# Inner rows of the gate and up products moved into the output stage of a transformer block: pieces between attention's products, Silu built from Exp, operands in two steps, layernorm in place

## The chip, the core and the metric

The kernel runs on one core of a Trainium2 chip. Its engines each work through their own instructions in order: TensorE (PE) for matmuls, VectorE (DVE) and ScalarE (ACT) for elementwise work and for reading the matmul banks (PSUM), GpSimd (POOL) for elementwise work, SyncE (SP) mainly for issuing transfers. The metric is the device time of one launch in microseconds (us); all data is float32.

## What is computed

Two sequences of 1024 tokens with 1024 features go through attention and a gated feed-forward block. Both are modulated by vectors that come from a small conditioning input. Cut to what matters here:

```python
h = layernorm(x) * (1 + ca) + sa
qkv = clip(h @ Wqkv.T, -8, 8)            # q and k are normalised, then 32 heads of 32
probs = softmax(q @ k.T * scale + alibi, causal)
x = x + ga * ((probs @ v) @ Wout.T)      # the output stage
h = layernorm(x) * (1 + cb) + sb         # called h2 in the kernel
gate = (h @ Wg.T) * ag                   # 2752 inner rows
up = (h @ Wu.T) * au
out = x + gb * (((silu(gate) * up) @ Wd.T) * ad)
```

## The kernel before

The inner dimension of 2752 is split. Five blocks of 512 (2560) run in the gate-and-up stage through two nested levels of a seven-product scheme (Strassen-Winograd). What is left, 192 inner rows, one full slice of 128 and one of 64, is called the rest. It is done with plain products, stored in `rest_dram`, and added in the down stage.

Tokens go in pairs of 128-row tiles: batch b, pair j from 0 to 3, eight pairs (b, j) in all.

**Order of the stages.** PE's instructions stand in program order (`matmul`, L763, while `pinned` is set). The other engines' instructions are placed by the framework's scheduler, so a DMA or a vector operation may stand ahead of where it is written.

1. Projections of batch 0 (`projections`, L943).
2. Attention of both batches (`attention`, L1029), interleaved with dense work (`dense_work`, L1500) by `together` (L1164). `together` walks through attention's units (96 of them for each batch) and runs dense work as long as its estimated time is below `share` (L1535). While batch 0's attention runs, the dense work is the projections of batch 1 with `side` (L1505), which takes one step of `down_weights` (L1204: load, four sums on POOL, store) at each of the products from the 24th on. While batch 1's attention runs, the dense work is the output stage of pairs (0,0) to (0,3), (1,0) and (1,1). `DENSE1` (L1356) is the estimated dense time spread over batch 1's attention.
3. After attention: the output stage of (1,2) and (1,3), together with all rest rows (`rest_rows`, L1377), and `second_batch` (L1335), which forms for each j the sums and differences of both batches' h2 that the gate-and-up stage needs, and sends them to `bop_dram` through `inner_b` (L1188).
4. Gate and up (L1824), then down (L1949).

**A unit of attention.** `scores` (L1052) issues four score matmuls (tile sc), then exponentials on ACT (L1085) that write p, and masks on POOL (L1089). `weigh` (L1095) issues the products with v (tile av) two units later, and adds p into the running sum on DVE or POOL (L1117). `settle` (L1119) multiplies the sum with ones. Scores have one buffer for each half, so the next unit's scores wait for the exponentials of this one.

**The output stage.** `operand` (L1244) loads the reciprocal softmax sums (rb) and four blocks of the attention output (aoA), multiplies them on DVE and POOL (L1264) and forms S1 to S4 (L1265 to L1269). `output` (L1274) calls it for a pair when the pair begins, unless it was made before. Then `seven` (L841) issues seven products of four matmuls, in chunks of two. `read` (L1296) takes each bank: copies on ACT (L1299), adds on DVE (L1305, L1307), products and adds into xr on POOL (L1308, L1309). The rows x1 are stored (L1314), normalised into a second tile xn (`normalize`, L719; the write is L747), transposed through a bank in four groups (`turned`, L861) and written, scaled, to h2 by DVE (L869).

**Pieces.** Transposes are put into a list (`Todo`, L876) and taken from it one at a time between chunks of the next pair. A piece takes a bank from `Banks.turn` (L784). During attention there is one such bank, shared with `settle`; `fresh` (L781) says whether it may be taken again. Each piece counts as 0.6 us for `together`.

**Rest rows.** For each pair three products of eight matmuls (tile rest, weights restw): gate of the slice of 128, up of the slice of 128, and both of the slice of 64 side by side. ACT applies Silu with the scale (L1392, L1393), DVE multiplies (L1396, L1399), SP stores (L1403, L1404). The h2 of six of the pairs is loaded back from memory for it (tile hl, `fetch`, L1550), and for `second_batch` too. Their weights are written after `output(0, ...)` in the program; the scheduler placed their loads ahead of the output weights (wB_o, wT_o).

Of the kernel before, what the change touches and what calls it, by code (L numbers as in the profile page):

```python
# [480 lines left out]
def kernel(  # L481
# [394 lines left out]
    class Todo:  # L876
# [18 lines left out]
        def add(self, go):  # L895
            self.list.append(go)

        def run(self, n, all_=False):
            self.place()
            for _ in range(min(n, len(self.list))):  # L900
                if not all_ and not self.banks.fresh():
                    return
                self.list.pop(0)(self.banks.turn())
                yield TURN
# [339 lines left out]
    def operand(b, j, ap_, own=None):  # L1244

        qb, y0 = 2 * j * P // QB, 2 * j * P % QB
        rb = ap_.tile([P, KC, 2 * P], FP, tag="rb", name=f"rb_{b}_{j}")
        for g in range(4):
# [7 lines left out]
                bufs=2 if q == "A21" and own is None else None,  # L1256
# [3 lines left out]
        for m, kh, q, eng in (  # L1260
            (0, 0, "A11", nc.vector), (0, 1, "A12", nc.gpsimd), (1, 1, "A22", nc.vector), (1, 0, "A21", nc.gpsimd),
        ):
            nc.sync.dma_start(a[q], ao_dram[b][qb][:, ds(kh * 4, 4), ds(y0 + m * P, P)])
            eng.tensor_mul(a[q], a[q], rb[:, ds(kh * 4, 4), ts(m, P)])  # L1264
# [5 lines left out]
        return a  # L1270
# [3 lines left out]
    def output(b, js, pools, banks, bt, todo, keep, made={}, q0=1):  # L1274
# [9 lines left out]
        for j in js:  # L1284
# [3 lines left out]
            a = made.get((b, j)) or operand(b, j, ap_)  # L1288
# [5 lines left out]
            part_t = {}  # L1294

# [15 lines left out]
            yield from seven(lambda q, i: a[q][:, i, :], bt, banks, read, todo.places(q0, 1), 2)  # L1311
# [3 lines left out]
            xn = []  # L1315
            for m in range(2):
                t_ = tkp.tile([P, D], FP, tag="xn", name=f"xn_{b}_{qts[m]}", bufs=2)
                xn.append(t_)
            todo.first(normalize(xs, xn, sm, f"f{b}_{j}"), b == 1 and j >= NJ // 2 - 1)
            h2 = keep(b, j)  # L1320
            for m in range(2):
                for g in range(2):
# [10 lines left out]
                    todo.add(go)  # L1333

# [21 lines left out]
    LEAD, DENSE0, DENSE1 = 16.0, 370.0, 136.0  # L1356
# [20 lines left out]
    def rest_rows(pairs, rest_w, pool, psp, tiles):  # L1377

        n1 = REST[1][1]
        ib = 4 * NSB  # L1380
        for b, j in pairs:
            hl = tiles[b, j].rearrange("p k h t -> p k (h t)")
            ps = []
            for r in range(3):
                bank = psp.tile([P, 512], FP, tag="rp", name=f"rest_{b}_{j}_{r}")[:, 0:256]
                for k in range(KC):
                    matmul(bank, rest_w[r][:, k, :], hl[:, k, :], start=(k == 0), stop=(k == KC - 1))
                ps.append(bank)
                yield 3.4
            sg = pool.tile([P, 2, 256], FP, tag="rsg", name=f"rsg_{b}_{j}")  # L1390
            ac = pool.tile([P, 2, 256], FP, tag="rac", name=f"rac_{b}_{j}")
            nc.scalar.activation(sg[:, 0], ps[0], AF.Silu, scale=vt[:, R_AG + ib : R_AG + ib + 1])  # L1392
            nc.scalar.activation(  # L1393
                sg[64 : 64 + n1, 1], ps[2][0:n1], AF.Silu, scale=vt[0:n1, R_AG + ib + 1 : R_AG + ib + 2]
            )
            nc.vector.scalar_tensor_tensor(  # L1396
                ac[:, 0], ps[1], vt[:, R_AU + ib : R_AU + ib + 1], sg[:, 0], ALU.mult, ALU.mult
            )
            nc.vector.scalar_tensor_tensor(  # L1399
                ac[64 : 64 + n1, 1], ps[2][64 : 64 + n1],  # L1400
                vt[64 : 64 + n1, R_AU + ib + 1 : R_AU + ib + 2], sg[64 : 64 + n1, 1], ALU.mult, ALU.mult,
            )
            nc.sync.dma_start(rest_dram[0][:, b, j], ac[:, 0].rearrange("p (h t) -> p h t", h=2))  # L1403
            nc.sync.dma_start(  # L1404
                rest_dram[1][0:n1, b, j], ac[64 : 64 + n1, 1].rearrange("p (h t) -> p h t", h=2)
            )
# [645 lines left out]
```

## Time and profile before

| what | us |
|---|---|
| median of 3 runs | 2902.21 (2901.19 to 2909.03) |
| the profiled execution, by the same clock as the runs | 2896.01 |
| its span, first to last instruction | 2894.3 |
| PE busy, share of the span | 2702.2, 93% |
| DVE, POOL, ACT busy | 1453.0, 1296.8, 685.2 |

The page shows the span in 40 equal slices of 72.4 us; each digit is a busy share in tenths, and PEclk the granted PE clock.

```profile
## 2 busy tenths in 40 slices
PE   6999999999997787878989999999999998999998
DVE  5766535665543356665554453454535346444442
ACT  1322244444443555545110011010101100000000
POOL 3312033345655565556457364464735541222342
PEclk9999999999998899999999999999999999999999
DMA  9878763756557444342687667585766659555542
```

Slices 13 to 19 are attention of batch 1 with the output stage between its products (about 907 to 1380 us); slices 20 to 22 hold the work behind it and the start of gate and up. The groups of instructions give the durations of the operations concerned: line, engine, operation, tiles, shape, count, then busy time and mean ns of one, then the idle time of the engine ahead of them.

```profile
L763 PE MATMUL rest<-hl,restw 128*128 128x256 f32 x288 | 65.3, 384 | 0.0
L763 PE MATMUL rest<-h2t,restw 128*128 128x256 f32 x96 | 21.6, 380 | 0.5 <-DVE rac L1396 0.5
L1392 ACT ACTIVATE rsg<-rest,vt x8: 473/473/474, 1400.7 to 1546.3; 128x256 f32<-128x256 f32 x8
L1396 DVE SCALAR_TENSOR_TENSOR rac<-rest,vt,rsg x8: 471/481/484, 1403.7 to 1556.5; 128x256 f32<-128x256 f32 x8
L1138 DVE RECIPROCAL rc<-rc x4: 935/947/953, 572.4 to 1389.2; 128x128 f32<-128x128 f32 x4
L869 DVE TENSOR_SCALAR h2t<-bank,modt 128x128 f32<-128x128 f32 x128 | 43.7, 402 | 25.0 <-PE bank L766 24.8
```

Each float32 matmul leaves two records, so 384 records of rest are 192 matmuls, 24 products. (In the three lines with "x8:" and "x4:" the numbers are the least, median and greatest ns, then the first and last start in us.)

### The profile page before, as it was taken

How to read it: one execution, taken by the hardware profiler on the slowest of the kernel's cores; microseconds unless marked ns; L12 is line 12 of the kernel's file. 1: busy time of each engine (PE TensorE's matmuls, PEld its weight loads, DVE VectorE, ACT ScalarE, POOL GpSimd, SP SyncE). 2: the span in 40 equal slices, each digit the busy share in tenths (PEclk: the TensorE clock that was granted, in tenths of full speed). 3: DMA queues.
4: the chain of work that ended last, by engine and by line, in shares of the span. 5: the costliest groups of instructions: out<-in, count | busy, mean ns of one | idle time of the engine just before them, and what ended most of it. 6: DMA issues, size and time to landing. Idle time of an engine off the chain costs nothing.

```text
span 2894.3 us, 29930 instructions
## 1 busy us (share of the span) xinstructions
PE 2702.2 (93%) x10271; PEld 1330.2 (46%) x10271; DVE 1453.0 (50%) x2285; ACT 685.2 (24%) x1523; POOL 1296.8 (45%) x1270
## 2 busy tenths in 40 slices
PE   6999999999997787878989999999999998999998
PEld 2444433333332222222655444444444446888776
DVE  5766535665543356665554453454535346444442
ACT  1322244444443555545110011010101100000000
POOL 3312033345655565556457364464735541222342
PEclk9999999999998899999999999999999999999999
DMA  9878763756557444342687667585766659555542
GB/s 342 311 270 311 284 219 117 236 181 220 191 164 236 130 153 134 124 124 77 208 262 241 211 225 235 169 285 160 268 190 206 229 169 286 158 146 146 158 144 81
DMA packets 377573, 579.14 MB, mean 200 GB/s; under 512 B 21590, under 2 KB 278712, under 8 KB 366276
## 3 DMA queue, kind: packets, MB, share of 16 engines
q1 hardware_dynamic: 363928, 556.12, 59.2%
q10 hardware_dynamic: 13484, 21.02, 2.2%
q8 instruction: 84, 1.38, 0.2%
q14 instruction: 77, 0.63, 0.1%
HBM read 411.89 MB, written 165.17 MB: 199 GB/s over the span
## 4 chain that ended last, share of the span: by engine, by line
PE 43%; DMA 4%; DVE 3%; issue 3%; POOL 3%; ACT 1%; SPq 0%; POOLq 0%; DVEq 0%; ACTq 0%
PE gx L1824 7%; PE ux L1824 7%; PE dx L1949 7%; PE gy L1824 6%; PE uy L1824 6%; PE dy L1949 5%; PE bank L763 1%; DMA bt<-bop_B 1%; DMA bop_T<-inner_T 1%; PE sc L763 1%; ACT p L1085 1%; DMA wuA<-in_L_ffn_Wu_dram 1%; PE rest L763 0%; PE av L763 0%; DVE asS L1778 0%
## 5 line engine op out<-in xcount | busy, mean ns | idle before, releaser
L1085 ACT ACTIVATE p<-sc,kw 128x128 f32<-128x128 f32 (+3 forms) x1024 | 421.6, 513 | 394.9 <-PE sc L763 376.7
L763 PE MATMUL bank<-wT,a 128*128 128x512 f32 x768 | 353.6, 603 | 12.0 <-DVE wT L832 6.8
L1117 POOL TENSOR_TENSOR p<-p,p 128x1024 f32<-128x1024 f32 (+3 forms) x128 | 262.1, 2048 | 183.4 <-PE av L763 157.5
L1117 DVE TENSOR_TENSOR p<-p,p 128x1024 f32<-128x1024 f32 (+3 forms) x192 | 246.2, 1291 | 153.4 <-POOL p L1089 97.3
L763 PE MATMUL bank<-wB,a 128*128 128x512 f32 x576 | 262.5, 601 | 1.2 <-DVE raw L982 0.6
L763 PE MATMUL sc<-cq,ck 32*128 32x512 f32 (+3 forms) x1536 | 194.5, 548 | 56.4 <-ACT p L1085 56.1
L1089 POOL TENSOR_SCALAR_AFFINE_SELECT p<-p 128x256 f32<-128x256 f32 x256 | 139.3, 556 | 200.8 <-ACT p L1085 194.7
L763 PEld LDWEIGHTS bank<-wT,a 128*128 128x128 f32 x768 | 140.0, 192 | 186.2 <-issue 168.9
L763 PE MATMUL av<-p,cv 128*32 128x512 f32 (+3 forms) x1536 | 173.2, 514 | 17.2 <-POOL p L1089 17.2
L763 PEld LDWEIGHTS bank<-wB,a 128*128 128x128 f32 x576 | 104.5, 190 | 145.0 <-issue 123.6
L763 PEld LDWEIGHTS sc<-cq,ck 32*128 32x128 f32 x1536 | 64.5, 186 | 193.6 <-ACT p L1085 103.0
L1824 PE MATMUL gy<-bt,sig 128*128 128x512 f32 x280 | 132.4, 595 | 10.7 <-DMA bt<-bop_B 5.7
L1824 PE MATMUL uy<-bt,siu 128*128 128x512 f32 x280 | 131.6, 592 | 0.0
L1824 PE MATMUL gx<-bt,sig 128*128 128x512 f32 x280 | 131.6, 592 | 0.0
L1824 PE MATMUL ux<-bt,siu 128*128 128x512 f32 x280 | 131.6, 592 | 0.0
L763 PEld LDWEIGHTS av<-p,cv 128*32 128x32 f32 x1536 | 34.0, 110 | 138.7 <-issue 80.7
L1824 PEld LDWEIGHTS gy<-bt,sig 128*128 128x128 f32 x280 | 52.4, 190 | 80.8 <-issue 71.1
L763 PE MATMUL bank<-wB_o,aoA 128*128 128x512 f32 x128 | 68.3, 667 | 18.7 <-DVE aoS L1266 17.7
L1824 PEld LDWEIGHTS uy<-bt,siu 128*128 128x128 f32 x280 | 53.2, 190 | 67.0 <-issue 65.8
L1824 PEld LDWEIGHTS ux<-bt,siu 128*128 128x128 f32 x280 | 53.2, 190 | 67.0 <-issue 65.5
L1824 PEld LDWEIGHTS gx<-bt,sig 128*128 128x128 f32 x280 | 53.2, 190 | 67.0 <-issue 65.7
L1824 PE MATMUL ux<-bt,wuS 128*128 128x512 f32 x160 | 75.2, 592 | 0.0
(415 smaller groups left out, 4467.9 us busy)
## 6 DMA issues: line engine op xcount, KB each, us to landing
bt<-bop_T SPq DMA_DIRECT2D x140, 512.0 KB
bt<-bop_B SPq DMA_DIRECT2D x99, 512.0 KB
a<-hop SPq DMA_DIRECT2D x20, 1792.0 KB
wm<-in_L_wmod_dram SPq DMA_DIRECT2D x48, 512.0 KB
wB<-in_L_attn_Wqkv_dram SPq DMA_DIRECT2D x21, 1024.0 KB
aq_S<-act_S SPq DMA_DIRECT2D x16, 1280.0 KB
qk<-qs SPq DMA_DIRECT2D x16, 1024.0 KB
act_S<-asS SPq DMA_DIRECT2D x30, 512.0 KB
```

What stands on the lines that cost most here:

```text
L763: return in_order(nc.tensor.matmul(*args, **kw_))
L1085: last_exp[0] = nc.scalar.activation(p[:, g, lo:hi], sp[:, g, lo:hi], AF.Exp, bias=kw[:, d, h_ : h_ + 1])
L1089: last_mask[0] = nc.gpsimd.affine_select(out=p[:, :, 0:P], in_=p[:, :, 0:P], pattern=[[0, 2], [1, P]], compare_op=ALU.is_ge, fill=0.0, bas ...
L1117: adders[b](half, jb).tensor_add(dst, dst, ps[half][:, :, 0:n])
L1824: nc.tensor.matmul(ps.rearrange("p (j t) -> p j t", j=NJ), ins[mat][qa][:, c2, :], bt[:, :, c2, :], start=(q in ("P1", "P2", "P5") and c2 ...
L1949: nc.tensor.matmul(bank[c_], ins[qa][:, s, :], wt[qb_][:, s, :], start=(q in ("P1", "P2", "P5") and s == 0), stop=(s == NSB - 1), skip_gro ...
```

## The change

- `rest_rows` goes. `rest_pieces` puts the three products of a pair into the list of pieces, behind the pair's transposes, with 3.5 us each in the estimate, and with two entries that take no bank and only issue the elementwise work. All eight pairs do it; six are in the part of the output stage that is dense work. The products read h2 from where it was just written.
- Silu is no longer called there. ACT takes the gate from the bank with its scale (Identity) and applies Exp to its negative; DVE limits, adds one, takes the reciprocal and multiplies twice. The scaled up rows go through a tile of the constants, `sc`, that is free by then. Exp, Ln and Identity are in the table that attention uses.
- `operand` has two steps. During a pair's third product the next pair's loads are issued, during its seventh its elementwise work. Block A22 gets a second buffer, as A21 had.
- The rows are normalised in place: xn is xr. The pool tok has four buffers of xr instead of three and two of xn.
- The rest weights are allocated ahead of the operand pool and loaded ahead of the output stage, on SP.
- `side` begins at the 12th product instead of the 24th; `DENSE1` goes from 136 to 190.
- After attention, the pieces left of (1,1) run with three more banks, then (1,2) and (1,3) are done one behind the other. The h2 of batch 0's pairs and of (1,0), (1,1) is still loaded for `second_batch`.

```diff
 class Todo:
-        def add(self, go):
-            self.list.append(go)
+        def add(self, go, us=TURN):
+            self.list.append((go, us))
         def run(self, n, all_=False):
             self.place()
-            for _ in range(min(n, len(self.list))):
+            while n and self.list:
+                go, us = self.list[0]
+                if us is None:
+                    go()
+                    self.list.pop(0)
+                    continue
                 if not all_ and not self.banks.fresh():
                     return
-                self.list.pop(0)(self.banks.turn())
-                yield TURN
+                self.list.pop(0)
+                go(self.banks.turn())
+                n -= 1
+                yield us
...
 def operand(b, j, ap_, own=None):
...
-                bufs=2 if q == "A21" and own is None else None,
+                bufs=2 if q in ("A21", "A22") and own is None else None,
...
+        for m, kh, q, eng in blocks:
             nc.sync.dma_start(a[q], ao_dram[b][qb][:, ds(kh * 4, 4), ds(y0 + m * P, P)])
+        yield
+        for m, kh, q, eng in blocks:
             eng.tensor_mul(a[q], a[q], rb[:, ds(kh * 4, 4), ts(m, P)])
...
 def output(...):
+            def ahead(e):
+                if e == 2 and nxt not in made and not step and (nxt[0], 2 * nxt[1] * P // QB) in settled:
+                    step[0] = operand(*nxt, ap_)
+                    next(step[0])
+                elif e == 6 and step and nxt not in made:
+                    next(step[0])
...
-            yield from seven(lambda q, i: a[q][:, i, :], bt, banks, read, todo.places(q0, 1), 2)
+            yield from seven(lambda q, i: a[q][:, i, :], bt, banks, read, todo.places(q0, 1, ahead), 2)
...
-            xn = []
-            for m in range(2):
-                t_ = tkp.tile([P, D], FP, tag="xn", name=f"xn_{b}_{qts[m]}", bufs=2)
-                xn.append(t_)
+            xn = xs
...
+            if rest is not None:
+                rest_pieces(b, j, todo, h2, *rest)
...
-    LEAD, DENSE0, DENSE1 = 16.0, 370.0, 136.0
+    LEAD, DENSE0, DENSE1 = 16.0, 370.0, 190.0
...
+    def rest_pieces(b, j, todo, h2, rest_w, pool):
+        n1 = REST[1][1]
+        hl = h2.rearrange("p k h t -> p k (h t)")
+        tiles = {}
+        def scaled(dst, ps, vec, r, rows_):
+            ib = vec + 4 * NSB + r
+            nc.scalar.activation(dst, ps, AF.Identity, scale=vt[rows_, ib : ib + 1])
+        def product(w, bank):
+            ps = bank[:, 0:256]
+            for k in range(KC):
+                matmul(ps, w[:, k, :], hl[:, k, :], start=(k == 0), stop=(k == KC - 1))
+            return ps
+        def gate(ps, r, lo, hi):
+            g, e = (pool.tile([P, 256], FP, tag=nm, name=f"{nm}_{b}_{j}_{r}") for nm in ("rg", "re"))
+            scaled(g[hi], ps[lo], R_AG, r, lo)
+            nc.scalar.activation(e[hi], g[hi], AF.Exp, scale=-1.0)
+            tiles[r] = g, e
+        def up(ps, r, hi):
+            scaled(urow[hi], ps[hi], R_AU, r, hi)
+        def act(r, hi, n):
+            g, e = tiles[r]
+            nc.vector.tensor_scalar(e[hi], e[hi], FAR, 1.0, ALU.min, ALU.add)
+            nc.vector.reciprocal(e[hi], e[hi])
+            nc.vector.tensor_mul(g[hi], g[hi], e[hi])
+            nc.vector.tensor_mul(g[hi], g[hi], urow[hi])
+            nc.sync.dma_start(rest_dram[r][0:n, b, j], g[hi].rearrange("p (h t) -> p h t", h=2))
+        every, lo, hi = slice(0, P), slice(0, n1), slice(64, 64 + n1)
+        urow = sc.rearrange("p k c -> p (k c)")
...
+        todo.add(lambda bank: gate(product(rest_w[0], bank), 0, every, every), 3.5)
+        todo.add(lambda bank: up(product(rest_w[1], bank), 0, every), 3.5)
+        todo.add(lambda: act(0, every, P), None)
+        todo.add(last, 3.5)
+        todo.add(lambda: act(1, hi, n1), None)
...
-                if 7 * n + e >= 24:
+                if 7 * n + e >= 12:
                     next(steps, None)
...
-            for n, k in (("oga", 1), ("tok", 3), ("opart", 1), ("osmall", 1), ("ao", 1))
+            for n, k in (("oga", 1), ("tok", 4), ("opart", 1), ("osmall", 1), ("restw", 1), ("ao", 1))
...
-        yield from output(0, range(NJ), *out_args, made)
-        right["w"] = rest_weights(rwp, nc.sync)
+        out_args.append((rest_weights(rwp, nc.sync), rwp))
+        yield from output(0, range(NJ), *out_args)
...
+    banks.others = banks.others + [rps.tile([P, 512], FP, tag=f"rq{i}", name=f"rq{i}") for i in range(3)]
...
-    with_turns(rows((0, 0), (1, 0)))
+    alone(todo.run(len(todo.list), True))
     fetch(1, 1)
-    def between():
-        yield from rows((0, 1))
-        second(0)
-        yield from rows((1, 1))
-    together(
-        between(), output(1, range(NJ // 2, NJ), *out_args, made, 3), lambda a: 0.6 * OUT_US / 2 * a / 20.6
-    )
+    second(0)
+    alone(output(1, range(NJ // 2, NJ), *out_args[:5], 5, out_args[6]))
+    second(1)
     in_range(rest_pool, rps)
     fetch(0, 2)
-    second(1)
     fetch(0, 3)
-    with_turns(rows((0, 2), (1, 2)))
     second(2)
-    alone(rows((0, 3), (1, 3)))
+    alone(todo.run(len(todo.list), True))
```

## The prediction

> **What bounds the kernel now.** I read three views: busy time by stretches, for the stages; the timeline of TensorE (PE) in two of them; the waits of PE. The cuts come from the timeline: 897 is the last matmul before the output stage, 1380 the end of attention, 1546 the first matmul of the gate-and-up stage.
>
> ```profile
> 895.00:916.00 21.00, 3.30 (x20) 0.71 (x18) 4.67 (x6) 2.62 (x5) 3.54 (x3) 0.68 0.98 268
> 916.00:1380.00 464.00, 381.51 (x2161) 123.12 (x2161) 257.79 (x356) 239.45 (x576) 278.44 (x250) 0.93 0.43 134
> 1380.00:1546.00 166.00, 153.88 (x579) 105.91 (x578) 91.77 (x178) 22.32 (x35) 76.28 (x64) 0.98 0.76 243
> ```
>
> Columns: stretch, length, busy PE, weight loads, VectorE (DVE), ScalarE (ACT), GpSimd (POOL), PE clock, DMA share, GB/s. In 464 us of attention over batch 1 no engine is full. In the 166 us behind it PE is nearly full, and DMA at 0.76.
>
> ```profile
> PE sc L763 <- ACT p L1085: 46.8, 41, 3.7
> PE bank L763 <- DVE aoS L1266: 17.7, 1, 17.7
> PE av L763 <- POOL p L1089: 17.2, 7, 5.1
> PE bank L763 <- DVE h2t L869: 15.2, 2, 8.6
> ```
>
> These are all of PE's long waits in 907 to 1379. The first is the attention loop itself: scores of a unit cannot start until ACT has read those of the unit before. The second is one stall at the stage's start.
>
> ```profile
> 1348.83 1.22 PE L763 MATMUL sc<-cq,ck 32*128 32x512 f32 x8
> 1349.98 0.43 PE L763 MATMUL av<-p,cv 128*32 128x128 f32 x8
> 1352.57 1.78 PE L763 MATMUL sc<-cq,ck 32*128 32x512 f32 x8 [2.17 <-ACT p L1085]
> ```
>
> A unit of 512 columns with no filler takes 3.7 us from scores to scores, of which PE works about 2. With one output chunk of 1.98 us (1346.91 is one) it takes about 4.0.
>
> ```profile
> 1392.50 10.52 PE L763 MATMUL rest<-hl,restw 128*128 128x256 f32 x48
> 1499.53 10.53 PE L763 MATMUL rest<-hl,restw 128*128 128x256 f32 x48
> 1546.12 1.88 PE L1824 MATMUL gx<-bt,wgA 128*128 128x512 f32 x4
> ```
>
> A pair's three inner-row products cost PE 10.5 us, 3.45 each. Twenty-four of them, 83 us, fill half of the stage behind attention.
>
> **What the Trainium skill says.** *TensorE: Matmul & The Clock Gate*, "What's actually happening": the PE clock falls to half after an idle window of about 3.4 us. The trace agrees: clock 0.68 around the stall, and the first chunk after it takes 3.67 us against 1.98. *ScalarE: Activation LUTs*, "What ACT_TABLE_LOAD costs": 1283 ns, with a drain 2.66 us; the trace shows 1.28 for the load. *VectorE: DVE Perf Modes*, "First, the fixed hardware budget": reciprocal is an iterative divide; here 128x128 takes 947 ns against about 285 for a tensor-tensor of that shape.
>
> **Part 1, the start of the output stage.** PE stands from 898.3 to 915.98. On SP's queue the last down-weight stores (888), operand loads (901 to 906.7) and wB_o (906.95) go one behind another; DVE's S2 ends at 915.9. With `side` at 12 the down-weight steps are over twelve products earlier. In the built order of the changed kernel the operand loads of (0,0) stand ahead of the last chunk loads, and wB_o follows the last stores of v, so it can issue at about 897.5, when the last projection matmul frees its space. Its load and the next are then the limit: 4 to 5 us. PE resumes at about 902.5 instead of 916: 13 us gained. Bounds: 6, if 1.5 MB more of rest weights and the 7 MB of wB_o crowd each other (DMA share is 0.98 here already), and 18, the whole stall with its slow first chunk. The earlier POOL work lies under batch 0's products, where PE is 91 to 99% busy and POOL 39 to 65% (stretches of 80 us from 440 to 840): nothing.
>
> **Part 2, pieces inside attention.** The built order gives the placement. Of 24 products 14 stand ahead of the last attention matmul: four pairs of batch 0 and two products of (1,0). Between score groups (101 of them) 28 intervals had no filler and 17 will have none; 12 of the 14 pieces have an interval to themselves, 2 share one with a chunk.
> - An interval of a piece alone: 1.07 + 1.00 + 3.45 = 5.5 us against 3.65, so 12 x 1.85 = 22 us.
> - Two on top of a chunk: 2 x 3.45 = 7 us.
> - Intervals with two chunks go from 8 to 13, with one from 61 to 53: 5 x 1.9 less 8 x 0.35 = 7 us.
> - ACT: six operations of 0.47 for each pair where two stood later; they come when the piece ends, under PE's next groups: nothing. DVE: `act` has two reciprocals of 256 columns, about 1.85 each (twice 947 less overhead, an estimate), and six small operations, about 6 us for each pair. DVE has 206 us free, but the softmax sums, the bank reads and the L869 reads that free the single shared bank queue behind: 4 us.
> - Operands in two steps: DVE waits 13.1 us at L1264 in the middle of the stage, 7.68 of it on the chain at 1247. Loaded a pair's half ahead this goes, but PE shows little of it: minus 5.
> - Layernorm in place: the write-back now waits for the x1 store, and SP, in order, puts that behind chunk loads. The normalisation is issued behind the next pair's first products: +1 to +2.
> Sum: attention gets 36 us longer, and I take off 4 for a clock above 0.93 as long gaps close: 32. Bounds: 15, if the 46.8 us of waits on ACT swallow most of the 48.3 us of pieces; 55, if nothing is swallowed and DVE adds 7.
>
> **Part 3, behind attention.** Ten products stay: 34.5 us instead of 82.8. Counted from attention's end:
> - rest of (1,1) and one piece: 15 us. Then nothing fills: last matmul to normalised rows took 7.7 us (1392.5 to 1400.2); plus 2 for the x1 store, 1.5 for the rows, 6 for four groups of reads at 1.37. Pieces of (1,1) run from 32 to 42.5. The operand of (1,2) is ready at about 34 (softmax sums at 10, rb loads at 24).
> - two pairs of products, 48.2, two groups of transposes, 2.4, waits of 3: up to 96. Before, this point was 1499.4, or 119.
> - pieces of (1,2) 10.4, beside the last normalisation. Before, that took from 1499.4 to 1510.27, with 3.84 us of table loads in it; now 7, plus 2 for the store, 1.5 and 6: 16.5. Pieces of (1,3): gate-and-up starts at 123.
> - its weights issue on ACT's queue when the last output matmul frees their space (1499.62 before), its sixth bt tile was issued by 1523.5, 24 us later: no stall of its own. SP has the stores of third and second pair, four weight tiles and bt still to issue. I expect it just late for the seventh tile: 4 us.
> So 127 against 166: 39 gained. Bounds: 20, if DMA binds (40.35 MB moved in those 166 us at 243 GB/s; in 127 us it would be 318, and the best 20 us slices show 323 to 329), and 48, the pieces alone.
>
> **Sum.** -13 + 32 - 39 = -20 us: 2876 against the profiled execution's 2896.01 (span 2894.3). The median of the runs shown is 2902.21, 6 above it; on that scale 2882. Gate-and-up and down stages keep their work.
>
> **Rivals.**
> - Everything is absorbed: attention +18, start -15, tail -48: 2857. For it, 82 us of PE waits in the loop; against it, a piece of 3.45 us does not fit a gap of 1.6.
> - DMA takes PE's place behind attention: tail -20, total -1: 2901. For it, share 0.76 and one SP queue in order with 40 MB; against it, some stores may slip under the first gate-and-up products.
> - Slower. Attention's loop stretches by the full length of the pieces: ACT reads a piece from the shared bank only in its turn behind exponentials, PE, in order, waits for that bank with transposes and sums behind it, and DVE's divides hold the reads. Attention +55, tail -30, start -10: +15, 2917. It decides from 50 us of stretching at a tail of 39. For it, PE already lost 15.2 us on that bank (L869); against it, 11 intervals that stood empty take pieces.
>
> **How the numbers follow.** A measurement tells about 0.3%, 9 us, from no change. Forecast (-20, plus or minus 12) 0.50; absorbed 0.14; DMA 0.17; slower 0.19. Faster: 0.95 of the first, all of the second, 0.4 of the third, 0.05 of the fourth: 0.69. Slower: a quarter of the third, three quarters of the fourth: 0.18; the same 0.13. The range 2854 to 2914 cuts about half of each outer case; most of the chance has one sign, so it stands alone.
>
> **What would show it.** Right: the first output matmul within 8 us of the last projection matmul; attention from there 25 to 40 us longer; attention's end to the first gate-and-up matmul near 127 us, with a PE gap of about 17 us ahead of the pieces of (1,1); no table load before gate-and-up. Wrong: PE waits on ACT or DVE for the shared bank above 30 us in attention; gate-and-up waiting for bt or weights by over 10 us; a start still held by wB_o.

## The result, and the profile after

The changed kernel takes 2884.05 us, median of 9 runs (2880.18 to 2893.61), beside 2905.58 for the kernel before, also 9 runs. The ratio is 0.9928, with a 95% interval of 0.9913 to 0.9942: about 21 us faster, 17 to 25. The forecast was 2882 and "faster". The total is right; the way to it is not, and the stages show that.

Line numbers move by a few: L1085 (exponentials) is L1093 now, L1089 (masks) L1097, L1264 (operand products) L1276, L747 and L869 stay, L1824 (gate and up) is L1857. The pieces are tile restw on h2t; L1415 is ScalarE's read of a piece, L1434 to L1437 are VectorE's part of the Silu, L1438 the store.

I cut both executions at the same points of TensorE's timeline and compare lengths, not absolute times: the code up to the first score matmul is the same in both, and took 360.8 us before and 366.2 after.

| stage, us | before | after |
|---|---|---|
| first scores to the end of the last projection matmul | 535.4 | 534.9 |
| from there to the first output matmul (the stall) | 19.8 | 6.0 |
| attention of batch 1, to its last matmul | 464.0 | 461.1 |
| attention's end to the last output matmul's end | 119.6 | 97.4 |
| from there to the first gate-and-up matmul | 46.5 | 57.0 |
| gate-and-up to the end of the program | 1348.2 | 1359.6 |

Busy time by stretches of the kernel after, in the columns of the prediction's first fence (length, PE, weight loads, DVE, ACT, POOL, PE clock, DMA share, GB/s):

```profile
907.00:1368.00 461.00, 417.88 (x2396) 160.75 (x2396) 289.31 (x395) 251.62 (x604) 262.62 (x248) 0.97 0.46 142
1368.00:1465.70 97.70, 79.59 (x228) 43.27 (x227) 66.94 (x107) 8.24 (x19) 48.59 (x36) 0.90 0.65 201
1465.70:1522.70 57.00, 29.37 (x117) 24.02 (x116) 45.79 (x79) 4.25 (x11) 37.91 (x37) 0.73 0.85 296
```

Attention carries 36 us more of PE's work (417.9 us busy against 381.5) in 3 us less. Behind it PE stands a lot: it is busy 29 of the 57 us ahead of gate-and-up. In the page's 40 slices of the kernel after the same is seen at slices 20 to 22 of PE: 7, 5, 8, where before they were 9, 8, 9.

PE's waits in attention of the kernel after (waited-for engine, us in total, times, longest) answer to the four lines of the prediction:

```profile
PE sc L763 <- ACT p L1093: 26.7, 26, 3.8
PE bank L766 <- DVE h2t L869: 5.4, 5, 2.9
PE bank L766 <- DVE xr L747: 4.6, 2, 3.8
...
PE av L763 <- POOL p L1097: 0.3, 1, 0.3
```

The pieces took 20 us of the waits for exponentials (46.8 to 26.7), which is what they were put there for. But two waits went that have nothing to do with pieces: POOL's masks (17.2 to 0.3) and the shared bank's reads (15.2 to 1.8, with 5.4 more ahead of transposes). The experiments ask which part of the change did that.

PE's waits behind attention of the kernel after:

```profile
PE rq L763 <- DVE h2t L869: 16.4, 2, 15.9
PE rq L766 <- DVE xr L747: 13.7, 1, 13.7
PE gx L1857 <- POOL wgS L1711: 8.4, 1, 8.4
PE rq L766 <- ACT sc L1415: 6.9, 1, 6.9
PE bank L763 <- DVE h2t L869: 4.8, 1, 4.8
```

Fourteen products went out of this part, and there are 50 us of waits in it now, where the kernel before had 15. The chain of waits over this stretch shows what stands behind the longest of them (start, us, what):

```profile
1453.39 6.43 DMA xr<-_attn_hidden_states_dram
1460.29 4.53 DMA bop_B<-hl
1472.64 5.47 DMA bop_T<-inner_T
1478.14 10.41 DMA bop_T<-hl
1488.56 7.86 DMA hl<-h
1496.44 1.75 DVE hl L1371
1507.54 2.55 DVE inner_T L1205
1510.10 1.92 DVE h2t L869 x6
```

From 1453 to 1496 us every long step is a transfer, 35 of the 43 us: input rows (xr) coming in, operands of gate-and-up (bop) going out, h2 of an earlier pair (hl) coming back. DVE's sums on it stand ahead of the reads (L869) that PE waits for.

One number settles the balance. From attention's last matmul to the end of the program the kernel before takes 1514.3 us and the kernel after 1514.0. The first 220 us of it, in the kernel before and in the kernel after:

```profile
1380.00:1600.00 220.00, 205.06 (x697) 128.17 (x696) 116.54 (x212) 30.61 (x48) 125.92 (x131) 0.98 0.77 246
1368.00:1588.00 220.00, 165.87 (x470) 92.18 (x469) 135.83 (x221) 23.06 (x46) 129.00 (x131) 0.86 0.75 242
```

With 39 us less of PE's work there, nothing was gained; the transfers moved 246 and 242 GB/s.

### The profile page after: what moved, and what is told of

The parts are those of the page before. It is cut to its first block, busy times and chain, and to the rows that moved or that the text cites. A ratio compares the mean times of both kernels' runs of the same rounds, so it can differ in the third digit from the quotient of the medians.

```text
span 2882.3 us, 29978 instructions
## 1 busy us (share of the span) xinstructions
PE 2698.3 (94%) x10271; PEld 1332.1 (46%) x10271; DVE 1506.3 (52%) x2333; ACT 689.3 (24%) x1548; POOL 1288.6 (45%) x1270
## 4 chain that ended last, share of the span: by engine, by line
PE 76%; DVE 7%; DMA 6%; issue 4%; POOL 3%; ACT 2%; SPq 0%; POOLq 0%; ACTq 0%; DVEq 0%
PE bank L763 24%; PE gx L1857 8%; PE ux L1857 8%; PE dx L1982 7%; PE gy L1857 6%; PE uy L1857 6%; PE dy L1982 5%; PE sc L763 5%; PE av L763 4%; ACT p L1093 2%; DVE p L1125 2%; DMA wm<-in_L_wmod_dram 1%; DMA xt<-_attn_hidden_states_dram 1%; PE bank L766 1%; DMA bt<-bop_B 1%
## 5 line engine op out<-in xcount | busy, mean ns | idle before, releaser
L1093 ACT ACTIVATE p<-sc,kw 128x128 f32<-128x128 f32 (+3 forms) x1024 | 421.6, 513 | 364.9 <-PE sc L763 354.2
L1125 DVE TENSOR_TENSOR p<-p,p 128x1024 f32<-128x1024 f32 (+3 forms) x192 | 252.1, 1325 | 130.7 <-POOL p L1097 78.7
L1097 POOL TENSOR_SCALAR_AFFINE_SELECT p<-p 128x256 f32<-128x256 f32 x256 | 127.9, 511 | 207.3 <-ACT p L1093 202.8
L763 PE MATMUL av<-p,cv 128*32 128x512 f32 (+3 forms) x1536 | 167.2, 507 | 1.4 <-issue 1.0
L1857 PE MATMUL gx<-bt,sig 128*128 128x512 f32 x280 | 133.5, 599 | 8.4 <-POOL wgS L1711 8.4
L1857 PE MATMUL gy<-bt,sig 128*128 128x512 f32 x280 | 132.3, 595 | 8.5 <-DMA bt<-bop_B 5.2
L1857 PE MATMUL ux<-bt,siu 128*128 128x512 f32 x280 | 132.3, 595 | 0.0
L1857 PE MATMUL uy<-bt,siu 128*128 128x512 f32 x280 | 131.6, 592 | 0.0
L1857 PEld LDWEIGHTS gx<-bt,sig 128*128 128x128 f32 x280 | 53.6, 192 | 76.2 <-issue 66.8
L1857 PEld LDWEIGHTS gy<-bt,sig 128*128 128x128 f32 x280 | 52.6, 190 | 78.1 <-issue 71.2
L1857 PEld LDWEIGHTS ux<-bt,siu 128*128 128x128 f32 x280 | 53.7, 192 | 67.9 <-issue 65.8
L1857 PEld LDWEIGHTS uy<-bt,siu 128*128 128x128 f32 x280 | 53.2, 190 | 66.9 <-issue 66.5
L763 PE MATMUL bank<-h2t,restw 128*128 128x256 f32 x272 | 68.0, 407 | 8.4 <-DVE h2t L869 6.6
L1857 PE MATMUL gx<-bt,wgS 128*128 128x512 f32 x160 | 75.2, 592 | 0.0
```

The lines of the kernel that those rows point to most:

```text
L763: return in_order(nc.tensor.matmul(*args, **kw_))
L1093: last_exp[0] = nc.scalar.activation(p[:, g, lo:hi], sp[:, g, lo:hi], AF.Exp, bias=kw[:, d, h_ : h_ + 1])
L1097: last_mask[0] = nc.gpsimd.affine_select(out=p[:, :, 0:P], in_=p[:, :, 0:P], pattern=[[0, 2], [1, P]], compare_op=ALU.is_ge, fill=0.0, bas ...
L1125: adders[b](half, jb).tensor_add(dst, dst, ps[half][:, :, 0:n])
L1857: nc.tensor.matmul(ps.rearrange("p (j t) -> p j t", j=NJ), ins[mat][qa][:, c2, :], bt[:, :, c2, :], start=(q in ("P1", "P2", "P5") and c2 ...
```

## The experiments

Each kernel is the changed one, or the one before, with the edit shown. The table gives the stages as above from one profile each; "end" is from attention's last matmul to the program's end. The ratio is to the kernel before, measured on the same chip, with its 95% interval.

| kernel | stall | attention | to last output matmul | to gate-and-up | end | median us | ratio |
|---|---|---|---|---|---|---|---|
| before | 19.8 | 464.0 | 119.6 | 46.5 | 1514.3 | 2905.58 | 1 |
| after | 6.0 | 461.1 | 97.4 | 57.0 | 1514.0 | 2884.05 | 0.9928 (0.9913, 0.9942) |
| one_step | 6.1 | 465.3 | 97.2 | 54.2 | 1514.7 | 2889.94 | 0.9944 (0.9927, 0.9961) |
| side_24 | 12.0 | 459.3 | 97.4 | 56.8 | 1511.5 | 2892.00 | 0.9960 (0.9944, 0.9976) |
| thin_pieces | 6.2 | 447.0 | 95.0 | 53.3 | 1512.1 | 2869.38 | 0.9876 (0.9859, 0.9892) |
| tail_order | 6.2 | 464.4 | 96.9 | 39.4 | 1514.1 | 2885.12 | 0.9931 (0.9913, 0.9949) |
| a22_single | 6.1 | 473.9 | 98.5 | 53.0 | 1513.7 | 2893.68 | 0.9956 (0.9939, 0.9972) |
| rg_two | 6.3 | 461.1 | 97.5 | 51.2 | 1511.9 | 2887.08 | 0.9942 (0.9922, 0.9961) |
| tail_rg | 6.0 | 465.4 | 97.6 | 37.8 | 1510.1 | 2883.00 | 0.9927 (0.9910, 0.9943) |
| no_divide0 | 6.1 | 464.3 | 97.2 | 56.5 | 1512.0 | 2884.07 | 0.9925 (0.9913, 0.9938) |
| before_inplace | 22.8 | 452.0 | 116.7 | 46.8 | 1516.1 | 2893.62 | 0.9959 (0.9941, 0.9977) |
| all_but_pieces | 19.4 | 433.9 | 121.0 | 46.0 | 1515.5 | 2871.24 | 0.9888 (0.9872, 0.9905) |
| best_place | 6.0 | 429.6 | 121.2 | 45.8 | 1516.5 | 2856.19 | 0.9842 (0.9822, 0.9861) |
| best_two | 6.0 | 431.3 | 122.0 | 46.7 | 1517.6 | 2856.36 | 0.9837 (0.9818, 0.9857) |

The kernels after, side_24, tail_order, rg_two and tail_rg have the same pieces and operands in attention, and their attention ran from 459.3 to 465.4. So one profile tells attention's length to within about 6 us, and smaller differences of it are not read. The stall repeats better: it is 6.0 to 6.3 in the ten kernels that have it short.

### The operand's two steps: one_step

```diff
-            yield from seven(lambda q, i: a[q][:, i, :], bt, banks, read, todo.places(q0, 1, ahead), 2)
+            yield from seven(lambda q, i: a[q][:, i, :], bt, banks, read, todo.places(q0, 1), 2)
```

> The changed kernel with the operand of each pair made in one piece at the pair's start again, as before the change. Theory (the operand in two steps is what lets attention take the pieces, because GpSimd's masks no longer queue behind operand products that wait for their loads): GpSimd waits again about 60 us for its operand products in attention over batch 1 (61 before the change, 2 with it), TensorE waits 15 us or more for masks, and attention takes 15 to 25 us longer than its 461 us; total 2899 to 2909 where the changed kernel has 2884. Rival (the pieces go into idle time whatever the operand does): attention at most 6 us longer, total below 2891.

Attention took 465.3 and the total's interval overlaps that of the changed kernel. My theory fell: POOL stands less than 4 us at operand products, and masks hold PE for 0.3 us, as in the changed kernel. The traces show why: in both kernels SP issues the operand loads (L1273) at the same times after the first output matmul, at 22, 65, 75, 115 and 150 us for example, to about 1 us over the first 230 us. The scheduler places the loads, not the line on which they are written. best_two beside best_place says the same from the other side (431.3 and 429.6).

### The second buffer of A22: a22_single, and the layernorm in place: before_inplace

```diff
-                bufs=2 if q in ("A21", "A22") and own is None else None,
+                bufs=2 if q == "A21" and own is None else None,
```

> The changed kernel with one buffer for operand block A22 instead of two, as before the change; all else stays, the two steps of the operand too. Theory (with one buffer the next operand's A22 cannot load until the pair's last product, and GpSimd's masks stand behind operand products that wait for it: 61 us of such waits before the change, 2 after it): GpSimd waits 30 us or more for operand products again, and attention takes 10 to 18 us longer than 461; total 2894 to 2902. Rival (the second buffer does nothing by itself): attention within 4 us of 461, total within 5 us of the changed kernel's 2884.

Attention 473.9, 12.8 us longer than in the changed kernel, and the total 2893.68, 9.6 us longer: the time came as expected (the total 0.3 us below the range). The sign I gave for it did not. POOL's long waits for operand products stayed away, and what grew was spread out: waits for normalised rows (4.6 to 8.5 us), POOL's waits for exponentials (48.5 to 61.3), a clock of 0.95 instead of 0.97. So the buffer is worth some 10 to 13 us beside the pieces, but this run does not show by which wait.

```diff
-            xn = []
-            for m in range(2):
-                t_ = tkp.tile([P, D], FP, tag="xn", name=f"xn_{b}_{qts[m]}", bufs=2)
-                xn.append(t_)
+            xn = xs
...
-            for n, k in (("oga", 1), ("tok", 3), ("opart", 1), ("osmall", 1), ("ao", 1))
+            for n, k in (("oga", 1), ("tok", 4), ("opart", 1), ("osmall", 1), ("ao", 1))
```

> The kernel before with the layernorm in place as the only part (four row buffers instead of three and two). Theory (the second A22 buffer is worth the 13 us that its removal cost the changed kernel, the rest of the 30 us is the layernorm in place): attention 445 to 452 us instead of 464, total 2884 to 2893. Rival (without the second A22 buffer nothing is gained): attention 460 us or more, total 2899 or more.

Attention 452.0: 12 us gained by this part alone. The total, 2893.62, lies 0.6 us above the range; the stall was 22.8 in this profile. SP's waits for an xr buffer whose rows were still being normalised turn into shorter ones for the transposes (the kernel before, then this one; us, times, longest):

```profile
SPq L1292 <- DVE xn L747: 31.0, 5, 9.4
SPq L1292 <- PE bank L766: 21.8, 8, 6.8
```

POOL's waits at operand products fall from 40 to 17 us in attention, and PE's wait for the shared bank's reads from 15.2 to 5.1.

### Everything but the pieces: all_but_pieces

The kernel before with the in-place edit above, two buffers for A22, and `side` from the 12th product. The second A22 buffer was not tried alone in the kernel before.

> The kernel before with three parts of the change: down-weight steps from product 12, two buffers for A22, layernorm in place. The inner rows stay where they were before, behind attention, with their own Silu. Theory (these parts, not the pieces, shorten attention, and the pieces cost about 0.4 of their length there): attention 440 to 448 us instead of 464, the stall at the start of the output stage 6 to 12 us instead of 19.8, the 166 us behind attention unchanged; total 2868 to 2880, so no slower than the changed kernel. Rival (attention gets shorter only because the pieces fill its gaps and keep the clock up): attention 458 us or more, total 2890 to 2898.

Attention 433.9, better than expected, and the total 2871 is 13 us below that of the changed kernel. PE's waits in attention of all_but_pieces, the stall with them:

```profile
PE sc L763 <- ACT p L1085: 45.8, 42, 3.8
PE bank L763 <- DVE aoA L1264: 17.3, 1, 17.3
PE bank L763 <- DVE h2t L869: 4.5, 1, 4.5
PE av L763 <- POOL p L1089: 4.0, 4, 2.1
```

The waits for exponentials are as they were (46.8 before): no piece fills them. The two others went from 17.2 and 15.2 to 4.0 and 4.5, 24 of the 30 us. In the kernel before they come about like this (timeline of the kernel before; in brackets the idle time ahead and its releaser):

```profile
1094.59 1.27 POOL L1264 TENSOR_TENSOR aoA<-aoA,rb 128x512 f32<-128x512 f32 x1 [10.15 <-DMA rb<-rec]
...
1095.88 2.84 DVE L1264 TENSOR_TENSOR aoA<-aoA,rb 128x512 f32<-128x512 f32 x1 [3.35 <-POOL aoA L1264]
...
1104.41 1.35 DVE L869 TENSOR_SCALAR h2t<-bank,modt 128x128 f32<-128x128 f32 x4
...
1105.82 1.08 PE L763 MATMUL bank<-p,ones 128*32 128x512 f32 x4 [8.59 <-DVE h2t L869]
```

POOL stands for 10 us at an operand product whose load is late, DVE behind it, and 10 us later the read of a transpose comes, for which PE has waited 8.59. The other such wait of PE, 6.65 us at 1013.06, stands behind DVE's own 10.95 us at L1264. The Trainium skill, *Perfetto Trace Analysis*, "Tensor Engine Instruction (MATMUL, LD_WEIGHTS)", calls ACT, DVE and GpSimd strict first-in-first-out; here that is the price: POOL stood 61 us at L1264 in the kernel before, 21.6 of them in the stall at the start, and about 2 at L1276 after the change. For the masks the link is weaker: PE's longest wait for them, 5.08 us at 1338.28, comes behind the operand's sums on POOL (L1268, L1269) and not behind a late load, and it is still there in before_inplace.

The surprise is the stall: 19.4 with `side` at 12. The earlier down-weight steps do not remove it here.

### The stall at the start: side_24 and best_place

```diff
-                if 7 * n + e >= 12:
+                if 7 * n + e >= 24:
```

> The changed kernel with the down-weight steps starting at product 24 again instead of 12. Theory (the later start of these steps made the stall at the output stage's start): 18 to 20 us from the last projection matmul's end to the first output matmul instead of 6.1, total 10 to 14 us longer. Rival (the new order of the operand loads, or the space that the layernorm in place frees, removed the stall): at most 9 us between them, total within 4 us of the changed kernel.

12.0: between the two, and the total is 8 us longer than the changed kernel's. So of the 13.7 us by which the change shortened the stall, the earlier steps bring 6; the other 8 went with `side` still at 24. best_place adds to all_but_pieces only the order in which space is taken:

```diff
-            for n, k in (("oga", 1), ("tok", 4), ("opart", 1), ("osmall", 1), ("ao", 1))
+            for n, k in (("oga", 1), ("tok", 4), ("opart", 1), ("osmall", 1), ("restw", 1), ("ao", 1))
...
-        rwp = ost.enter_context(tc.tile_pool(name="restw", bufs=1))
```

> The kernel before with four parts of the change: down-weight steps from product 12, two buffers for A22, layernorm in place, and the space of the rest weights taken ahead of that of the operands (so the operands' space lies elsewhere). Inner rows behind attention as before. Theory (the place of the operands' space decides when the first operand can load, and with the earlier down-weight steps this removes the stall; the three parts without it left 19.4 us): 6 to 8 us from the last projection matmul to the first output matmul, attention 430 to 438 us, total 2855 to 2862. Rival (the stall went with the earlier rest weights and their use in the output stage, not with the place): 17 us or more, total 2868 to 2874.

6.0 us, and 2856 in all. SP's timeline shows why. All_but_pieces loads the rest weights early and the first operand (rb, aoA) when it is already needed:

```profile
837.39 0.37 SPq L1371 DMA_DIRECT2D restw<-in_L_ffn_Wg_dram  x1
...
906.82 1.82 SPq L1249 DMA_DIRECT2D rb<-rec  x4
908.68 7.10 SPq L1263 DMA_DIRECT2D aoA<-ao  x4
```

Best_place has the operand's loads at that time, some 55 us ahead of need, as the kernel after has:

```profile
841.54 1.81 SPq L1249 DMA_DIRECT2D rb<-rec  x4
...
846.07 8.16 SPq L1263 DMA_DIRECT2D aoA<-ao  x6
```

In all_but_pieces SP's last wait ahead of rb is 3.7 us for v<-raw, a store out of a tile of the last projections. So with the rest weights' space taken first, the operands' space lies where its last user is done earlier; with `side` at 12 SP's queue is also free to use it (in side_24 SP stands 21.7 us for POOL at a down-weight store, and the first operand's rb follows only at 893.9). Old place: 19.8 with `side` at 24, 19.4 at 12. New place: 12.0 and 6.0. Two steps of these four kernels are one edit each: the place is worth 13 us with the early steps (all_but_pieces to best_place), and the early steps are worth 6 us in the new place (side_24 to the kernel after). The 8 us between old and new place with the late steps lie between kernels that differ in much else, so what the place alone is worth there is not shown.

best_two adds the two steps to it:

> As best_place, and the operands in two steps, the loads during the third and the products during the seventh product of the pair before. Theory (the scheduler moves the loads forward by itself; the two steps were worth 4 us in attention beside the pieces): attention 0 to 5 us shorter than in best_place, total up to 5 us shorter. Rival (loads moved up push other transfers of SP's order back): attention 0 to 5 us longer.

Attention 431.3 beside 429.6, ratios 0.9837 and 0.9842: no difference that can be told.

### What the pieces cost: thin_pieces and no_divide0

best_two has every part of the change in attention but the pieces (and `DENSE1` at 136). So the pieces' price stands in two lines of busy time by stretches. best_two first, then the kernel after:

```profile
907.00:1338.40 431.40, 376.43 (x2161) 121.20 (x2161) 253.55 (x355) 240.28 (x576) 272.22 (x248) 0.94 0.47 146
```

```profile
907.17:1368.28 461.11, 418.16 (x2397) 160.79 (x2397) 289.31 (x395) 251.62 (x604) 262.62 (x248) 0.97 0.46 142
L763 PE MATMUL bank<-h2t,restw 128*128 128x256 f32 x224 | 55.3, 403 | 3.6 <-DVE h2t L869 1.8 <-DVE rs L1135 1.7
```

PE has 41.7 us more to do, and attention is 29.7 us longer: 12 us of it went into time that PE stood, 55 us in best_two and 43 in the kernel after. The pieces themselves keep PE busy for 55.3 us (the last line). So the rest of PE's work took some 14 us less than in best_two, at a granted clock of 0.97 instead of 0.94; the ratio of the two clocks, taken of best_two's 376 us, gives 12 us, an estimate. About half of the pieces' length was absorbed, as much by work that ran faster as by time in which PE had stood.

```diff
         def product(w, bank):
-            for k in range(KC):
-                matmul(ps, w[:, k, :], hl[:, k, :], start=(k == 0), stop=(k == KC - 1))
+            ks = range(KC) if b else range(1)
+            for k in ks:
+                matmul(ps, w[:, k, :], hl[:, k, :], start=(k == 0), stop=(k == ks[-1]))
```

> The changed kernel with seven of the eight matmuls of every inner-row product of batch 0 left out; all the reads, Silu steps and stores stay. That is 12 products x 7/8 x 3.45 us = 36 us of TensorE less in attention over batch 1. Theory (the pieces lie in time in which TensorE stood): attention at most 8 us shorter than 461. Rival (the step of the prediction: a piece costs 1.85 us net where it is alone and its whole 3.45 us on top of a chunk, 29 us for 14): attention some 22 us shorter.

14.1 us shorter, between the theory and the rival. Fourteen whole products at that rate, 14.1 x 14/12 x 8/7, are 19 us of the 30, an estimate that carries the 6 us by which one profile of attention differs from the next.

```diff
-            nc.vector.tensor_scalar(e[hi], e[hi], FAR, 1.0, ALU.min, ALU.add)
-            nc.vector.reciprocal(e[hi], e[hi])
-            nc.vector.tensor_mul(g[hi], g[hi], e[hi])
-            nc.vector.tensor_mul(g[hi], g[hi], urow[hi])
+            if b:
+                nc.vector.tensor_scalar(e[hi], e[hi], FAR, 1.0, ALU.min, ALU.add)
+                nc.vector.reciprocal(e[hi], e[hi])
+                nc.vector.tensor_mul(g[hi], g[hi], e[hi])
+                nc.vector.tensor_mul(g[hi], g[hi], urow[hi])
```

> The changed kernel with VectorE's part of the Silu left out for batch 0: the clamp, the reciprocal and the two multiplications of eight half steps, 26 us of VectorE in attention by the changed kernel's trace, with 27 us in which VectorE waits ahead of them for ScalarE or TensorE. The products, ScalarE's reads and the stores stay; what is stored for batch 0 is the scaled gate row. Theory (with the products alone costing 14 to 19 of the pieces' 30 us, VectorE's part is most of the rest, because the reads that free the shared bank and the softmax sums queue behind it): attention 8 to 14 us shorter than 461, total 2870 to 2876. Rival (the step of the prediction, which put VectorE's part at 4 us): attention 0 to 5 us shorter, total 2879 or more.

464.3 us and 2884.07: nothing. DVE had 24 us less to do in attention (289.3 to 265.7) and simply stood longer for PE. My theory fell; the term of 4 us in the prediction was too high, if anything. Of the other 11 us of the pieces' 30, two more output chunks inside attention than before (317 matmul records against 309, four to a chunk) are 4 us. The last 7 are not settled: ScalarE's reads and the other spacing of the chunks (`DENSE1`) were not tried by themselves.

### Behind attention: tail_order, rg_two, tail_rg

```diff
     alone(output(1, range(NJ // 2, NJ), *out_args[:5], 5, out_args[6]))
+    alone(todo.run(len(todo.list), True))
     second(1)
...
     second(2)
-    alone(todo.run(len(todo.list), True))
```

> The changed kernel with the rest of the todo list (transposes and pieces of the last pairs) run directly behind the output stage, ahead of the batch sums of pairs 1 and 2. Theory (VectorE's order, with the sums ahead of the reads of the transposes, makes TensorE stand behind the last output matmul): of the 57 us from the last output matmul's end to the first gate-and-up matmul 15 to 20 go; gate-and-up's wait for its weight sums, 8.4 us now, grows by up to 8; total 8 to 18 us shorter. Rival (the transfers bind there, DMA share 0.85): gate-and-up starts earlier but waits as much longer for weights and operands; total within 5 us.

The wait of 15.9 us went, and the 57 us fell to 39.4, as expected. The total did not move: the stage behind gave all of it back. Gate-and-up stood 9.4 us at the same place as in the kernel after and 11.9 at a new one. Timeline of tail_order at the new one:

```profile
1546.25 16.84 DVE L1202 TENSOR_TENSOR inner_T<-hl 128x256 f32<-128x256 f32 x1
...
1562.09 0.72 POOL L1724 TENSOR_TENSOR siu<-wuS,siu 128x256 f32<-128x256 f32 x1
1563.01 0.41 DVE L1204 TENSOR_TENSOR inner_T<-oo 128x256 f32<-128x256 f32 x1
...
1564.41 3.70 PE L1857 MATMUL gy<-bt,sig 128*128 128x512 f32 x4 [11.94 <-DVE gC L1666]
```

A VectorE sum that takes 0.41 us took 16.84. It lay beside POOL's gate-weight sums, which ran without a gap from 1535.45 to 1562.81, and ended 0.3 us after the last of them; behind it stood the read that frees gate-and-up's bank. The Trainium skill, *SBUF — State Buffer*, "Who interferes with whom", says that a VectorE instruction with two inputs in SBUF contends with GpSimd instructions that read SBUF, and that the one which comes second blocks. The trace agrees and shows more: VectorE's sum did not get through between the two dozen POOL instructions in a row. No run moved POOL's sums away, so that they are the cause is what the page and the timeline together say, not an experiment.

```diff
-    rest_pool = rest_st.enter_context(tc.tile_pool(name="rest", bufs=1, side="right"))
+    rest_pool = rest_st.enter_context(tc.tile_pool(name="rest", bufs=2, side="right"))
...
-    alone(output(1, range(NJ // 2, NJ), *out_args[:5], 5, out_args[6]))
+    alone(output(1, range(NJ // 2, NJ), *out_args[:5], 5, (out_args[6][0], rest_pool)))
```

> The changed kernel with two buffers for the gate rows and their exponential in the last two pairs (1,2) and (1,3). Theory (ScalarE reads the second gate piece of a pair only when the store of the first has landed, and SP issues that store late in its order; TensorE stands for it 6.9 us behind the output stage and 8.4 us inside gate-and-up): the 57 us from the last output matmul to gate-and-up shrink by 5 to 8, the wait of 8.4 us inside gate-and-up goes or falls below 3; total 8 to 15 us shorter than 2884. Rival (DMA or SP's order holds the next thing at the same time): total within 4 us.

The mechanism was right: the wait of 6.9 us fell to 1.7 and the one of 8.4 went (with one buffer ACT's read of the second piece had stood 10.54 us, released by the store of the first). The gain was not there: gate-and-up now stood 9.7 us for gC, behind another VectorE sum of 13.55 us.

Tail_rg has both edits:

> The changed kernel with both: the two buffers for the last pairs' gate rows, and the todo list run ahead of the batch sums of pairs 1 and 2. Theory: from the last output matmul to gate-and-up 32 to 36 us instead of 57 (39 with the order alone); in gate-and-up the 9.4 us wait goes, and the 11.9 us wait for a VectorE sum that ran 16.8 us beside GpSimd's weight sums stays; total 8 to 18 us shorter than 2884. Rival (transfers bind: DMA share 0.95 with the order alone): total within 4 us.

37.8 us to gate-and-up, three more waits for VectorE and operands of 12.0, 6.7 and 2.5 us behind it, total as before.

All three of my theories for this part named a real wait, and took it away, and none moved "end", which stays within 1510 to 1518 us in all fourteen kernels, with 24 products behind attention or 10. In the first 220 us behind attention tail_rg moves 241 GB/s with PE busy 169 us, best_place 242 with PE busy 204. That fits a stage whose pace is set by what has to be moved and summed there, not by PE. But equal rates over equal times say only that the same bytes were moved, and the transfers do not fill the stretch. Two windows of 60 us of the kernel after:

```profile
1388.30:1448.30 60.00, 50.79 (x143) 28.98 (x144) 39.23 (x69) 5.33 (x12) 27.72 (x22) 0.88 0.51 150
1448.30:1508.30 60.00, 33.42 (x119) 21.21 (x117) 47.52 (x78) 4.05 (x10) 39.10 (x38) 0.81 0.90 311
```

DMA is at 0.51 in the first and at 0.90 in the second. So besides the rate of the transfers there are other candidates: when their data are ready, the order of SP's one queue, and the sums of VectorE and POOL. No run took transfers or sums out or changed SP's order, and which of these sets the pace is open.

Where the lead is lost can be read. Counted from attention's last matmul, gate-and-up's first matmul starts at 166 us in the kernel before, 154 in the kernel after and 136 in tail_order and tail_rg. The 81st matmul record of gx and gy starts at 238, 234, 231 and 231. A lead of 12 to 31 us has shrunk to 4 to 8, little more than the 6 us by which profiles of attention differ.

## Why the prediction was right, and where it was wrong

- **Part 1** (13 gained, bounds 6 to 18): 13.7. PE resumed 6.0 us after the last projection matmul, against 6.3 predicted. The load of wB_o, issued at 901.2 and 902.3 us, fits as the limit, as said, but the profile names no releaser for PE's last 4 us. The cause was half wrong: the prediction had the down-weight steps do it and took the operand's early loads as their consequence. The steps bring 6 us in the new place of the operands' space; in the old place the stall stayed at 19.4. The edit in the diff is one pool moved in a list.
- **Part 2** (+32, bounds 15 to 55): -2.9, outside the bounds. Two terms failed. "Operands in two steps: minus 5" saw that late operand loads cost time, but priced the steps, which are worth nothing that can be told, and gave the second A22 buffer no price of its own; "layernorm in place: +1 to +2" had the wrong sign, since the prediction saw only the added wait and not the fourth xr buffer. In place alone took 12.0 us off attention (464.0 to 452.0), A22's buffer with it 18.1 more (433.9; that kernel also has `side` at 12, which made no difference to attention in side_24). I had read DVE's 13.1 us at L1264 and not POOL's 61 at the same line, nor what queues behind them, though 17.2 us for masks and 15.2 for the bank's reads stood in my own fence. The pieces' terms were near in sum: 22 + 7 + 7 for PE, 4 for DVE, -4 for the clock, 36 in all, against 30 measured. Singly they were not: DVE has nothing, the clock gave back some 12 to 14, and 7 of the 30 are unexplained.
- **Part 3** (-39, bounds 20 to 48): 0. Up to the last output matmul it was right: 97.4 us after attention's end, 96 predicted, and the gap ahead of the pieces of (1,1) was there (13.7 us of 17). Then two steps failed. The sum assumed that gate-and-up starts 27 us after the last output matmul; it took 57, with transfers and VectorE's sums ahead of the reads. And it gave gate-and-up 4 us of waiting; up to the program's end that stage and the next took 11 us more than before, 8 of them in the first 57 records of gx and gy. The prediction listed a small gain as a bound ("20, if DMA binds") and as the second rival; even that was too mild.
- **The sum**: -20 predicted, -13.7 - 2.9 - 0.3 = -17 by the stages, -17 to -25 by the runs. That is luck: an error of 35 us in attention and one of 39 behind it have opposite signs.
- **The signs** I named for "wrong" (shared bank above 30 us, gate-and-up waiting above 10) stayed quiet at about 10 and 8.4 us while two of three parts were wrong. The two signs with a stage's length in them (25 to 40 longer, 127 us) told it at once.
- **The change against its parts**: best_two, which keeps the rest rows and their Silu where they were, takes 2856 us, 0.9837 of before; the changed kernel 0.9928. What the pieces bring behind attention is nothing, and in attention they cost 30 us.

## What to carry to other kernels

Before work is moved out of a stage, ask whether anything else would keep that stage's length if the work were gone. Here PE was nearly full behind attention, and still 39 us less of its work shortened the program by nothing there, while the moved work cost 30 us where it went. In a change of several parts, price the buffers and the place of each pool as parts of their own: here they, with the earlier down-weight steps, are the whole gain. When a wait is traced to one engine's operand, look at the same line on every engine that runs it, and at what queues behind it there.

## What the runs showed of the hardware that I had not expected

- A VectorE tensor-tensor of 128x256 (0.41 us alone) took 13.55, 16.84 and 16.90 us in rg_two, tail_order and tail_rg while POOL ran tensor-tensors without a gap. In the kernel after, from 1502 to 1507 us, the same pair of operations took turns: 0.94 us on VectorE and 0.90 on POOL, against 0.41 and 0.72 alone. What decides between the two is not shown.
- A reciprocal of 128x256 and one of 64x256 take the same 1.75 us, and one of 128x128 takes 0.95: in these three the time goes by columns and not by rows, and the second 128 columns cost 0.80 us.
- The first 360 us, the same code in every kernel, took 361 to 367 us from profile to profile. Differences of that size between two spans say nothing about a change further down.
